# A four-layer graph network on one core: the end of layer 0 in one written order, row terms by sums, late searches in resident chunks' places

## The chip, the core and the metric

The kernel runs on one core of one Trainium2 chip. The metric is device time in microseconds of one execution. An execution is also recorded by the hardware profiler; its times are given from the start of its span. The engines are named PE (TensorE, with PEld for its weight loads), DVE (VectorE), ACT (ScalarE), POOL (GpSimd) and SP (SyncE, which here only issues transfers).

## The reference

`x` is 2708 x 128, `adj` is 2708 x 2708, all in float32. Four layers are applied, each as `x = x + layer(relu(layernorm(x)))`. Layers 0 and 1 are the ones that the change touches:

```
# layer 0: h = relu(layernorm(x)); d = 1/sqrt(rowsum(adj))
z  = leaky_relu(d * (adj @ (d * h)) @ W1 + b1, 0.1)
d2 = max(|z_i|^2 + |z_j|^2 - 2 z_i.z_j, 0)
S  = exp(-sqrt(d2 + 1e-10) / 2), kept for the 4 largest of each row, else 0
A2 = S + adj;  d' = 1/sqrt(rowsum(A2))
x  = x + d' * (A2 @ (d' * h)) @ W2 + b2

# layer 1: h = relu(layernorm(x)); XW = h @ W
s_col, s_row = XW @ a[:128], XW @ a[128:]
den = exp(leaky_relu(s_row_i + s_col_j, 0.01));  num = adj @ den
x  = x + adj @ ((den / num, 0 where num is 0) @ XW)
```

Layers 2 and 3 each multiply `adj` by `h` once more and apply dense weights.

## The kernel before, in words

Nodes are cut into T = 22 tiles of 128 (the last, T-1, has 20 rows) and into six groups of four tiles (the last group has tiles 20 and 21). `adj` comes in transposed, and a chunk is 128 of its rows, 1354 KB. Chunks pass through four rotating places (`big`, tag "big"); the last five, 17 to 21, stay resident in places of their own ("res17" to "res21"). All transfers of chunks go through SP's queue in program order.

Row sums: every chunk is multiplied by ones (L373), while layer 0's node products are made between the chunks (`weighted`).

`aggregate` (L272) is the loop of each multiplication by `adj`. For each chunk that isn't resident it makes six products into six PSUM banks (`acc0` to `acc5`; a float32 product of 128x512 is two passes in the profile); then it adds the resident chunks bank by bank, and calls `done(g)` for each finished bank. `kept` says how many of the last chunks stay in `big`, `back` from which chunk on missing resident chunks are read.

Search: for each tile a strip of 2708 similarities is made by PE (L512, L520), copied by ACT (L527), and searched by DVE: MAX8 finds the eight largest values (L529), FIND_INDEX8 their places (L531). From tile LATE = T-4 on, FIND_INDEX8 is put off (`find_last`, L549). The strips of tiles 18 and 19 lie in two spare places ("U", "Z"), the others in `big`. From the values come `sim`, `deg2`, `dinv2` and the scaled rows `y2` (L577, L579), which are also written to DRAM as `ydr` (L583).

The four nearest rows of each node are added by `add_near` (L600): per tile four indirect gathers from `ydr` on POOL (L604), each of 128 rows, and four DVE terms that add them, weighted by `simd`, to `xs` (L610). Tiles 0 to 14 are added ahead of the aggregation of `y2`, the others within its `done_l0` or after it. 23 buffers (`gath`) take the gathered rows.

`done_l0(g)` (L733) takes a finished bank: ACT copies it (`u2T`, L650), PE transposes it, DVE adds it to `xs` (`add_l0`, L644), and `layernorm_relu` (L203) makes `h1`: moments on DVE (L211, L212), the root on ACT (L213), reciprocal and scale on DVE (L214, L216), RELU on ACT (L221). Then layer 1's row term is made: for groups 0 to 3 by `terms` (L659: transposes of `h1` into `hT`, a product with `rep`, and transposes back), for groups 4 and 5 by `last_terms` (L675: a DVE product with `wrow` and a sum, then PE transposes that spread it into `row_all`). `column_terms` (L703) makes the column term from `hT`; `own_tiles` (L713) compares a group with itself.

Layer 1's attention goes by sorted places: `place(t)` (L813) makes a mask of `row_all` against tile t's row terms on DVE (L844), sums it on ACT (L845) and counts it on PE (L822); `places_of` turns counts into places, and POOL scatters them (L879). `node_terms` at t = 16 finishes the column terms. Between them `total` (L905) adds up chunks weighted by `w_n` (L913), the four of `big` and the five resident ones first, then 13 that are read again. Last, a loop over 22 steps (L1106) fetches rows of `adj` in sorted order into `mov` and writes a table of knots to DRAM.

The program's order on an engine is planned by a scheduler from program order and priorities; `pin(ins)` keeps an instruction in program order among the pinned ones of its engine.

Of the kernel before, what the change touches and what calls it, by code (L numbers as in the profile page):

```python
# [9 lines left out]
F32 = mybir.dt.float32  # L10
# [15 lines left out]
def kernel(  # L26
# [29 lines left out]
    def width(t):  # L56
        return TAIL if t == T - 1 else P
# [15 lines left out]
    def pin(ins):  # L73

        return tc.keep_in_program_order(ins)

    resident = {}
    pools = {}
# [117 lines left out]

    def acc(b):
        return ps_a.tile([P, 512], F32, name=f"acc{b}")

    def span(g):  # L200
        return slice(GROUPS[g][0] * P, min(GROUPS[g][1] * P, N))
# [133 lines left out]
    def weighted(g, part):  # L335
        t0, t1 = GROUPS[g]
        if part == 0:
            p = acc(g % 2)
            for t in range(t0, t1):
                o = (t - t0) * P  # L340
                mm = nc.tensor.transpose(
                    p[:, o : o + width(t)], h0[: width(t), t, :], ident[: width(t), : width(t)]
                )
                if t == t0:
                    pin(mm)
            nc.scalar.copy(h0T[:, span(g)], p[:, : span(g).stop - span(g).start])
            return
        dst, w = ((y1, w1), (hw2, w2))[part - 1]
        p = acc(2 * part + g % 2)
        for t in range(t0, t1):  # L350
            o = (t - t0) * P
            mm = nc.tensor.matmul(
                p[: width(t), o : o + P], h0T[:, cols(t)], w, start=True, stop=True
            )
            if t == t0:
                pin(mm)
        for a, e, n in ((t0, min(t1, T - 1), P), (max(t0, T - 1), t1, TAIL)):
            if a < e:
                (nc.scalar.copy, nc.vector.tensor_copy)[part - 1](
                    dst[:n, a:e, :],  # L360
                    p[:n, (a - t0) * P : (e - t0) * P].rearrange("p (t f) -> p t f", f=P),
                )

    for g in range(NG):
        layernorm_relu(h0, g)
    for i in range(T):
        c = chunk(i)
        w = width(i)
        if 3 <= i < 3 + 3 * NG:
            weighted((i - 3) // 3, i % 3)  # L370
        for b, (k0, n) in enumerate(KBS):
            g = 32 * (b % 4)
            nc.tensor.matmul(  # L373
                sums[b // 4][g : g + 32, :n],
                ones[:w, :32],
                c[:w, k0 : k0 + n],
                start=(i == 0),
                stop=(i == T - 1),
            )
        if i < FIRST:  # L380
            del resident[i]
    sum_rows = lay.tile([P, 1024], F32, name="sum_rows", tag="U")
    for half, p0, p1 in ((0, 0, 128), (1, 0, 32 * (NKB - 5)), (1, 32 * (NKB - 5), 32 * (NKB - 4))):
        n = KBS[4 * half + p0 // 32][1]
# [107 lines left out]
    top_v = res.tile([P, T, 8], F32, name="top_v")  # L492
    top_i = res.tile([P, T, 8], U32, name="top_i")

    LATE = T - 4
    strips = []
    nc.vector.memset(top_v[:, T - 1, :], 0.0)

    def strip(t):
        if LATE <= t < LATE + 2:  # L500
            return lay.tile([P, N], F32, name=f"strip{t}", tag="UZ"[t - LATE])
        return big.tile([P, N + 1], F32, name="strip", tag="big")[:, :N]

    for t in range(T):
# [62 lines left out]
    dinv2 = keep.tile([P, T], F32, name="dinv2")  # L567
    nc.scalar.activation(deg2s, deg2s, AF.Ln)
    nc.scalar.activation(dinv2, deg2s, AF.Exp, scale=-0.5)
    y2 = lay.tile([P, T, D], F32, name="y2", tag="Y")  # L570
    ydr = dram.tile([P * T, D], F32, name="ydr")
    for i in range(2):
        resident[i] = chunk(i)
    for t0, t1 in ((0, T // 2), (T // 2, T)):
        for t in range(t0, t1):
            if t % 5 in (1, 3):
                scaled = nc.scalar.mul(y2[:, t, :], hw2[:, t, :], dinv2[:, t : t + 1])  # L577
            else:
                nc.vector.tensor_scalar(  # L579
                    y2[:, t, :], hw2[:, t, :], dinv2[:, t : t + 1], None, op0=ALU.mult  # L580
                )
        pin(
            nc.sync.dma_start(  # L583
                ydr.rearrange("(p t) f -> p t f", t=T)[:, t0:t1, :], y2[:, t0:t1, :]
            )
        )
    with tc.issue_after(scaled.ins):
        nc.scalar.preload_act_table_set("sqrt_and_others")
    for t in (T - 2, T - 1, *range(LATE, T - 2)):
        find_last(t)  # L590
    row_numbers(P, LATE, T - 1)
    row_numbers(TAIL, T - 1, T)
# [4 lines left out]
        simd, sim, dinv2[:, :, None].to_broadcast([P, T, TOPK]), ALU.mult  # L597
    )

    def add_near(t, late=False):  # L600
        w = width(t)
        for k in range(TOPK):
            g = res.tile([P, D], F32, name="gath", bufs=23)
            nc.gpsimd.indirect_dma_start(  # L604
                out=g[:w, :],
                out_offset=None,
                in_=ydr[:, :],
                in_offset=bass.IndirectOffsetOnAxis(ap=near_u[:w, t, k : k + 1], axis=0),
            )
            term = nc.vector.scalar_tensor_tensor(  # L610
                xs[:w, t, :],
                g[:w, :],
                simd[:w, t, k : k + 1],
                xs[:w, t, :],
                op0=ALU.mult,
                op1=ALU.add,
            )
            if late and k == 0:
                pin(term)

# [6 lines left out]
    def vec(name, n=T, dt=F32):  # L629
        return keep.tile([P, n], dt, name=name)  # L630
# [17 lines left out]
    def to_x1(g, s2):  # L648
        k0, n = KBS[g]
        nc.scalar.copy(u2T[:, k0 : k0 + n], s2[g][:, :n])  # L650
        node_product(u2T, None, g, add_l0)
# [20 lines left out]
            )  # L672
        nc.vector.tensor_copy(r_nat[:, t0:t1], r_ps[0][:, t0:t1])

    def last_terms(g):  # L675

        t0, t1 = GROUPS[g]
        k0, n = KBS[g]
        prod = res.tile([P, 4, D], F32, name="prod")
        nc.vector.tensor_tensor(  # L680
            prod[:, : t1 - t0, :],
            h1[:, t0:t1, :],
            wrow[:, None, :].to_broadcast([P, t1 - t0, D]),
            ALU.mult,
        )
        e = min(t1, T - 1)
        nc.vector.tensor_reduce(r_nat[:, t0:e], prod[:, : e - t0, :], AX.X, ALU.add)
        if e < t1:
            nc.vector.tensor_reduce(
                r_nat[:TAIL, e:t1], prod[:TAIL, e - t0 : t1 - t0, :], AX.X, ALU.add  # L690
            )
        p = ps_s.tile([P, 512], F32, name="ps")
        for t in range(t0, t1):
            w = width(t)
            o = (t - t0) * P
            nc.tensor.transpose(
                p[:, o : o + w], r_nat[:w, t : t + 1].to_broadcast([w, P]), ident[:w, :w]
            )
        return nc.scalar.copy(row_all[:, k0 : k0 + n], p[:, :n])

    c_ps = []

# [25 lines left out]
            nc.vector.tensor_tensor(o, o, eq, ALU.subtract)  # L728


    late = {0: (15,), 1: (16,), 2: (17,), 3: (18, 19), 4: ()}

    def done_l0(g, s2):  # L733
        to_x1(g, s2)
        if g < NG - 1:
            layernorm_relu(h1, g)
            for t in late[g]:
                add_near(t, late=True)
        if 1 <= g < NG - 1:
            terms(g - 1)  # L740
        if g == NG - 1:
            last_terms(g - 1)
        if g > 2:
            column_terms(g - 3)
        if g in (2, 3):
            own_tiles(g - 2, res)

    for t in range(15):
        add_near(t)
    aggregate(y2, done_l0, lambda i: spread(y2, nc.sync) if i == 4 else None, kept=4)  # L750
    transposed(hT, h1, NG - 2, nc.scalar.copy)
    column_terms(NG - 3)
    for t in range(GROUPS[-1][0], T):
        add_near(t, late=True)
    layernorm_relu(h1, NG - 1)
    last_row = last_terms(NG - 1)
    transposed(hT, h1, NG - 1, nc.scalar.copy)
    column_terms(NG - 2)

    with tc.issue_after(last_row.ins):  # L760
        tables = nc.scalar.preload_act_table_set("natural_log_exp_and_others")
# [23 lines left out]
        return top  # L785

    rmax = node_max("rmax", r_nat, r_ps[0][:, 256:384])
    r_n = vec("r_n")
    nc.vector.tensor_scalar(r_n, r_nat, rmax, None, op0=ALU.subtract)
    w_n = vec("w_n")  # L790
# [130 lines left out]
    early = {todo[len(here) + n]: total_chunk(todo[len(here) + n], n) for n in range(2)}  # L921

    def node_terms():
        column_terms(NG - 1)
        nc.vector.tensor_copy(c_nat[:, : T - 1], c_ps[0][:, : T - 1])
        nc.vector.tensor_copy(c_nat[:TAIL, T - 1 :], c_ps[0][:TAIL, T - 1 : T])
        cmax = node_max("cmax", c_nat, c_ps[0][:, 384:512])
        nc.vector.tensor_scalar(cmx, cmax, rmax, -1.0, op0=ALU.add, op1=ALU.mult)
        c_n = vec("c_n")
        nc.vector.tensor_scalar(c_n, c_nat, rmax, None, op0=ALU.add)  # L930
        nc.vector.tensor_scalar(hb, c_n, 0.0, -0.495, op0=ALU.max, op1=ALU.mult)
        nc.scalar.activation(s_n, c_n, AF.Exp, scale=0.99)
        nc.scalar.activation(sig, hb, AF.Exp)
# [4 lines left out]
    for t in range(T):  # L938
        place(t)
        if t % 4 == 3 or t == T - 1:  # L940
            places_of(t // 4)
        if t in (2, 5, 8, 11):
            own_tiles(2 + t // 3, spare)
        if t == 16:
            node_terms()
        if 1 <= t <= len(here) + 4 or t in (15, 16, 18, 20):
            total(done)
            done += 1
# [124 lines left out]
            )  # L1073

    weights(0)


    xw = lay.tile([P, T, D], F32, name="xw", tag="Y")
# [299 lines left out]
```

## Time and profile before

| | us |
|---|---|
| three timed runs | 1194.0, 1194.6, 1188.3 |
| median | 1194.0 |
| the profiled execution | 1289.2 |
| its span | 1287.3 |
| row sums, to the first product of `aggregate(y1)` | 0 to 93.5 |
| `aggregate(y1)` and the search | 93.5 to 337.3 |
| `aggregate(y2)`, to the first finished bank | 337.3 to 506.4 |
| end of layer 0, to the first mask of `place` | 506.4 to 552.3 |
| places and totals, to the first table product | 552.3 to 619.7 |
| table, attention, layers 2 and 3 | 619.7 to 1287.3 |

A line of the timeline gives the start, the time of a run of like instructions, the engine, the line of the program, the operation, output and inputs, and how often; in brackets stands the idle time before it and what ended it. A row of the table of stretches gives the stretch, its length, the busy time and instructions of PE, PEld, DVE, ACT and POOL, PE's granted clock, the DMA share and GB/s. The slices of the page cut the span in 40, 32 us each.

### The profile page before, as it was taken

Reading aid. Unit: us, or ns where it says so; the run is one execution under the profiler, and the core shown is the slowest. Engines: PE = TensorE matmul, PEld = TensorE weight load, DVE = VectorE, ACT = ScalarE, POOL = GpSimd, SP = SyncE. Lnnn points to the kernel's source line nnn. Section 1 sums busy time; section 2 is a strip of 40 time slices with the busy share of each in tenths; the row PEclk is TensorE's granted clock in tenths of the full one; section 3 lists DMA queues with packets and bytes.
Section 4 is the critical chain, followed back from the end, with each engine's and each line's share of the span. In section 5 each row is a group of like instructions: output and inputs, shape, how many; then the busy total and the mean of one; then the engine's idle time right before and its main releaser. Section 6 shows DMA issues by size and latency. Waiting matters only on the chain. (4 is left out here: it accounts for less than half of the span.)

```text
span 1287.3 us, 10181 instructions
## 1 busy us (share of the span) xinstructions
PE 1056.8 (82%) x3603; PEld 499.3 (39%) x3603; DVE 561.4 (44%) x1177; ACT 409.7 (32%) x636; POOL 245.7 (19%) x211
## 2 busy tenths in 40 slices
PE   4879999999763379797677771787879999999998
PEld 1324444444221134454333330333334445545444
DVE  2020026999832001783466663899970012104003
ACT  3100014544300000475567644687840012003000
POOL 4000000000277700134211103577500000000000
PEclk9989999999875579788899896698889999999999
DMA  9997800001553361256999997999949945761841
GB/s 344 422 383 276 302 3 1 1 1 43 212 202 96 94 253 50 90 233 245 274 406 395 345 348 269 423 414 419 417 184 395 326 164 181 265 245 54 306 159 43
DMA packets 38800, 298.76 MB, mean 232 GB/s; under 512 B 6735, under 2 KB 9710, under 8 KB 12290
## 3 DMA queue, kind: packets, MB, share of 16 engines
q1 hardware_dynamic: 24798, 203.76, 42.0%
q0 software_dynamic: 13952, 94.36, 19.7%
q8 instruction: 28, 0.46, 0.1%
q14 instruction: 22, 0.18, 0.0%
HBM read 265.76 MB, written 32.87 MB: 232 GB/s over the span
## 5 line engine op out<-in xcount | busy, mean ns | idle before, releaser
L284 PE MATMUL acc<-chunk,y 128*128 128x512 f32 (+1 forms) x408 | 180.3, 591 | 74.7 <-issue 58.4
L1213 PE MATMUL acc<-hi,xw 128*128 128x512 f32 (+3 forms) x264 | 124.2, 634 | 57.8 <-DVE hi L1203 57.8
L1106 PE MATMUL acc<-mov,wt 128*128 128x512 f32 (+1 forms) x264 | 115.4, 592 | 40.7 <-DMA mov<-in_adj_dram,src_u 39.2
L284 PE MATMUL acc<-chunk,h 128*128 128x512 f32 (+1 forms) x384 | 148.3, 542 | 0.0
L604 POOL DMA_INDIRECT gath<-ydr,near_u x88 | 83.8, 952 | 337.5 <-DMA ydr<-y 245.9
L284 PEld LDWEIGHTS acc<-chunk,y 128*128 128x128 f32 x408 | 79.5, 205 | 175.5 <-issue 162.0
L512 PE MATMUL acc<-zT 128*128 128x512 f32 (+2 forms) x264 | 112.7, 559 | 0.4 <-ACT strip L527 0.3
L1213 PEld LDWEIGHTS acc<-hi,xw 128*128 128x128 f32 (+1 forms) x264 | 55.7, 220 | 126.3 <-issue 66.1
L1110 DVE COPY mov<-acc 2x512 f32<-2x512 f32 x126 | 74.3, 611 | 61.1 <-PE acc L1106 60.5
L284 PEld LDWEIGHTS acc<-chunk,h 128*128 128x128 f32 x384 | 68.6, 190 | 73.2 <-issue 73.1
L1106 PEld LDWEIGHTS acc<-mov,wt 128*128 128x128 f32 x264 | 52.1, 205 | 103.8 <-issue 82.3
L527 ACT COPY strip<-acc 128x512 f32<-128x512 f32 (+2 forms) x132 | 60.7, 556 | 61.0 <-issue 35.8
L284 PE MATMUL acc<-chunk,attended 128*128 128x512 f32 x192 | 73.1, 542 | 2.5 <-DMA chunk<-in_adj_dram 2.5
L1145 POOL DMA_INDIRECT lo<-table,lo_u x22 | 58.0, 2638 | 68.6 <-issue 41.1
L1111 ACT COPY knots<-acc 128x512 f32<-128x512 f32 x88 | 50.2, 590 | 62.9 <-DVE mov L1110 56.4
L1195 ACT ACTIVATE hi<-hi,lam 128x2708 f32<-128x2708 f32 (+3 forms) x24 | 56.5, 2363 | 35.6 <-issue 26.7
L1191 DVE SCALAR_TENSOR_TENSOR hi<-lo,lam,hi 128x2708 f32<-128x2708 f32 (+3 forms) x24 | 67.1, 2801 | 1.0
L1203 DVE SCALAR_TENSOR_TENSOR hi<-row_all,inv_s,hi 128x2708 f32<-128x2708 f32 (+3 forms) x24 | 67.0, 2797 | 0.4 <-ACT hi L1196 0.4
L512 PEld LDWEIGHTS acc<-zT 128*128 128x128 f32 (+1 forms) x264 | 45.0, 185 | 51.7 <-issue 41.9
L529 DVE MAX8 top_v<-strip 128x8 f32<-128x2708 f32 (+1 forms) x22 | 64.4, 2967 | 0.4 <-ACT strip L527 0.4
L650 ACT COPY u2T<-acc 128x512 f32<-128x512 f32 (+1 forms) x6 | 3.2, 533 | 168.3 <-PE acc L284 168.2
L1196 ACT ACTIVATE hi<-hi,hb 128x2708 f32<-128x2708 f32 (+3 forms) x24 | 56.5, 2361 | 0.7
(281 smaller groups left out, 1179.5 us busy)
## 6 DMA issues: line engine op xcount, KB each, us to landing
chunk<-in_adj_dram SPq DMA_DIRECT2D x108, 1354.0 KB
table<-knots SPq DMA_DIRECT2D x20, 1354.5 KB
res<-in_adj_dram SPq DMA_DIRECT2D x9, 1354.0 KB
chunkY<-in_adj_dram SPq DMA_DIRECT2D x2, 1354.0 KB
chunkU<-in_adj_dram SPq DMA_DIRECT2D x2, 1354.0 KB
res<-in_adj_dram SPq DMA_DIRECT2D x8, 211.6 KB
ydr<-y SPq DMA_DIRECT2D x2, 704.0 KB
gath<-ydr,near_u POOLq DMA_INDIRECT x88
```

The lines of the kernel that those rows point to most:

```text
L284: nc.tensor.matmul(out[b][:, :n], y[r, i, :], chunk(i)[r, k0 : k0 + n], start=(i == 0), stop=(i == T - 2),)
L512: mm = nc.tensor.matmul(zz[b][:w, :n], zT[:, cols(t)], zT[:, k0 : k0 + n], start=True, stop=False)
L527: copied = nc.scalar.copy(s[:w, k0 : k0 + n], zz[b][:w, :n])
L529: nc.vector.max(top_v[:w, t, :], s[:w, :])
L604: nc.gpsimd.indirect_dma_start(out=g[:w, :], out_offset=None, in_=ydr[:, :], in_offset=bass.IndirectOffsetOnAxis(ap=near_u[:w, t, k : k + ...
L1106: nc.tensor.matmul(p[:, :n], wt[:, t, :], moving[t][:, k0 : k0 + n], start=True, stop=True)
L1110: nc.vector.tensor_copy(moving[t + 1][:2, k0 : k0 + n], p[:2, :n])
L1145: nc.gpsimd.indirect_dma_start(out=dst[:w, :], out_offset=None, in_=table[:, :], in_offset=bass.IndirectOffsetOnAxis(ap=idx[:w, t : t + 1] ...
L1191: nc.vector.scalar_tensor_tensor(num, lo[:w, c], kap, num, op0=ALU.mult, op1=ALU.add)
L1195: nc.scalar.activation(num, num, AF.Ln, scale=sc)
L1203: nc.vector.scalar_tensor_tensor(att[:w, c], row_all[:w, c], inv_s[:w, t : t + 1], att[:w, c], op0=ALU.max, op1=ALU.mult,)
L1213: nc.tensor.matmul(py[b][:, :n], xw[:w, t, :], att[:w, k0 : k0 + n], start=(t == T - 1), stop=(t == T - 2),)
```

## The change

It has these parts.

- Row sums: chunk T-1 is taken ahead of T-2, and after each of the last six chunks PE makes three products of constants that nobody reads (`warm`).
- Search: LATE is T-5. The strips of tiles 17, 20 and 21 take the places of the resident chunks 17, 18 and 19, which are then dropped and read again in `aggregate(y2, ...)` from its sixth chunk on (`back=5`).
- 16 unread products follow the search; four chunks instead of two are asked for ahead of `ydr`, which is written in three parts instead of two.
- Tile T-1's gathers: the four lists of 20 rows are copied into one list of 128 (`near_p`, `simd_p`, at partitions 0, 32, 64 and 96) by eight small transfers from ACT's queue; one gather and one PE product with `four_w` take their place.
- End of layer 0: banks 4 and 5 are no longer worked off one by one in `done_l0`, but after the loop, in an order written out for PE, DVE and ACT (`Ordered` pins each instruction).
- Groups 3 to 5 get their row terms by sums; their `hT` and column terms are made after `rmax` and in `node_terms`, and `own_tiles(1)` moves to `place`.
- 14 unread products follow `weights(0)`, ahead of the table loop.

```
+    class Ordered:          # every call is pinned
+        def __getattr__(self, name):
+            return lambda *a, **k: pin(getattr(self.engine, name)(*a, **k))
+    pe, dve, act = Ordered(nc.tensor), Ordered(nc.vector), Ordered(nc.scalar)
...
+    def warm(p, n):
+        for _ in range(n):
+            pin(nc.tensor.matmul(p, ident_b, ident_b[:, None, :].to_broadcast([P, 4, P]), start=True, stop=True))
...
-    for i in range(T):
+    for n_, i in enumerate([*range(T - 2), T - 1, T - 2]):
...
+        if n_ >= T - 6:
+            warm(acc(0), 3)
...
-    LATE = T - 4
+    LATE = T - 5
...
     def strip(t):
-        if LATE <= t < LATE + 2:
-            return lay.tile([P, N], F32, name=f"strip{t}", tag="UZ"[t - LATE])
+        if t in (LATE, T - 2, T - 1):
+            i = T - L0_RES + (LATE, T - 2, T - 1).index(t)
+            del resident[i]
+            return res_rows.tile([P, N + 1], F32, name=f"strip{t}", tag=f"res{i}")[:, :N]
+        if t > LATE:
+            return lay.tile([P, N], F32, name=f"strip{t}", tag="UZ"[t - LATE - 1])
...
+    warm(acc(5), 16)
...
-    for i in range(2):
+    for i in range(4):
         resident[i] = chunk(i)
-    for t0, t1 in ((0, T // 2), (T // 2, T)):
+    for t0, t1 in ((0, 9), (9, 17), (17, T)):
...
+    near_p = res.tile([P, 1], U32, name="near_p")
+    simd_p = res.tile([P, 1], F32, name="simd_p")
...
+    for k in range(TOPK):
+        for dst, src in ((near_p, near_u), (simd_p, simd)):
+            nc.scalar.dma_start(dst[32 * k : 32 * k + TAIL, :], src[:TAIL, T - 1, k : k + 1])
...
+    def last_near():
+        g = gathered(near_p)
+        dve.tensor_scalar(four_w, four_w, simd_p, None, op0=ALU.mult)
+        p = ps_s.tile([P, 512], F32, name="ps")
+        pe.matmul(p[:TAIL, :P], four_w[:, :TAIL], g, start=True, stop=True)
+        return p
...
-    late = {0: (15,), 1: (16,), 2: (17,), 3: (18, 19), 4: ()}
+    late = {0: (15,), 1: (16,), 2: (17,), 3: (18,)}
+    complete = []
     def done_l0(g, s2):
+        if g >= NG - 2:
+            complete.append(s2[g])
+            return
         to_x1(g, s2)
-        if g < NG - 1:
-            layernorm_relu(h1, g)
-            for t in late[g]:
-                add_near(t, late=True)
-        if 1 <= g < NG - 1:
+        layernorm_relu(h1, g)
+        for t in late[g]:
+            add_near(t, dve)
+        if g:
             terms(g - 1)
-        if g == NG - 1:
-            last_terms(g - 1)
-        if g > 2:
-            column_terms(g - 3)
-        if g in (2, 3):
-            own_tiles(g - 2, res)
+        if g == 2:
+            own_tiles(0, res)
...
+    aggregate(y2, done_l0, ..., kept=4, back=5)
+    # E4, E5 = groups 4, 5: ACT copies both banks, PE transposes both
+    column_terms(0)
+    add_near(T - 3, dve)
+    x1(E4)
+    for t in range(*GROUPS[E4]):
+        moments(t)
+    roots(E4)
+    x1(E5)
+    normed(E4)
+    p = last_near()
+    prod = row_sums(E4 - 1)
+    natural(E4 - 1, prod)
+    as_row(E4 - 1)
+    column_terms(1)
+    column_terms(2)
+    dve.tensor_tensor(xs[:TAIL, T - 1, :], xs[:TAIL, T - 1, :], p[:TAIL, :P], ALU.add)
+    moments(T - 1)
+    add_near(T - 2, dve)
+    moments(T - 2)
+    roots(E5)
+    prod = row_sums(E4)
+    normed(E5)
+    natural(E4, prod)
+    as_row(E4)
+    natural(E5, row_sums(E5))
+    last_row = as_row(E5)
...
     rmax = node_max("rmax", r_nat, r_ps[0][:, 256:384])
+    for g in range(E4 - 1, NG):
+        transposed(hT, h1, g, nc.scalar.copy)
...
     def node_terms():
-        column_terms(NG - 1)
+        for g in range(E4 - 1, NG):
+            column_terms(g)
...
-        if t in (2, 5, 8, 11):
-            own_tiles(2 + t // 3, spare)
+        if t in (1, 2, 5, 8, 11):
+            own_tiles(1 + (t + 1) // 3, spare)
...
     weights(0)
+    warm(acc(5), 14)
```

`x1(g)` adds the transposed banks to `xs` on DVE; `moments(t)`, `roots(g)` and `normed(g)` are the steps of `layernorm_relu`, split so that they can be set in order; `row_sums`, `natural` and `as_row` are the steps of the former `last_terms`.

## The prediction

> **What bounds the kernel now.** I read the chip line first, then the slices, the groups, the timeline of each turn between stages, and the waits. The chain that ended last reaches back only to 921 us, so all that the change touches has to be read from the timeline. The slices show one stretch unlike the rest:
>
> ```profile
> ## 2 busy tenths in 40 slices
> PE   4879999999763379797677771787879999999998
> ...
> PEclk9989999999875579788899896698889999999999
> ```
>
> Slices 12 to 15 (about 370 to 480 us) are the second aggregation of layer 0 (`aggregate(y2, ...)`, L284), which should keep PE full. The table of stretches (PE, PEld, DVE, ACT, POOL busy, clock, DMA share, GB/s) says what happened:
>
> ```profile
> 337.00:369.00 32.00, 31.40 (x76) 14.43 (x76) 20.49 (x46) 3.96 (x10) 19.02 (x20) 0.93 0.79 301
> 369.00:461.00 92.00, 32.22 (x37) 10.54 (x37) 14.64 (x42) 0.00 (x0) 60.09 (x64) 0.52 0.30 91
> 461.00:501.00 40.00, 36.74 (x96) 17.24 (x99) 0.00 (x0) 0.00 (x0) 0.00 (x0) 0.96 0.62 243
> ```
>
> For 92 us PE took one product per 1.4 us instead of 0.43, with nothing to wait for ("issue"), and DMA idled. The same loop over layer 0's first matrix gives its normal length: its chunk part runs from 93.51 to 173.56, 80.05 us; here it runs from 337.28 to 500.71, 163.4 us. So this execution holds 83.4 us that a normal one doesn't. It took 1289.2 us, the three timed runs 1188 to 1195: 83.4 of the 95 us between are this stretch. I therefore read every time after it less 83.4 ("corrected"), and the sum below against 1289.2 - 83.4 = 1205.8, which stands 1% above the median of 1194; differences are carried over one to one. The correction matters: in the profile the gathers look free, since they finished while PE crawled; in a normal run they don't.
>
> The turn before it, from the search for the nearest rows to the aggregation:
>
> ```profile
> 325.17 5.84 DVE L529 MAX8 top_v<-strip 128x8 f32<-128x2708 f32 x2
> 327.30 0.38 PE L520 MATMUL acc<-sq_rows,ones_b 3*20 3x512 bf16 x2
> 331.40 2.96 DVE L529 MAX8 top_v<-strip 20x8 f32<-20x2708 f32 x1
> 337.28 31.40 PE L284 MATMUL acc<-chunk,y 128*128 128x512 f32 x76 [9.60 <-DVE y L579]
> 338.47 1.56 SPq L583 DMA_DIRECT2D ydr<-y  x2
> 344.20 1.03 POOL L604 DMA_INDIRECT gath<-ydr,near_u  x1 [245.88 <-DMA ydr<-y]
> ```
>
> DVE bounds the search: from the first MAX8 at 216.8 to 334.36 it never pauses, 40 instructions (22 MAX8, 18 FIND_INDEX8) of 2.94 us. PE and ACT are done with the last strip at 328.9. The end of the layer:
>
> ```profile
> 506.35 0.59 ACT L650 COPY u2T<-acc 128x512 f32<-128x512 f32 x1 [165.37 <-PE acc L284]
> ...
> 548.05 0.29 DVE L211 BATCH_NORM_STATS2 ln_st<-xs 128x6 f32<-128x128 f32 x1
> ...
> 552.28 1.56 DVE L844 TENSOR_SCALAR mask<-row_all,r_nat 128x2580 bf16<-128x2580 f32 x1 [0.78 <-ACT row_all L699]
> ```
>
> The first mask of layer 1 starts at 552.28, 45.9 us after the first finished bank; corrected, 422.9 and 468.9. PE's clock between 529 and 555 is 0.56: the chain DVE, ACT, PE is passed back and forth there, and none is full.
>
> **What the Trainium skill says.** "TensorE: Matmul & The Clock Gate", Part 1: an idle window of about 3.4 us halves PE's clock, and as long a busy one restores it. The trace agrees: after its 9.6 us of idleness at 337.28 the weight loads stand 0.85 us apart until 341.4, then 0.43; at 93.5 the same for 5.4 us. So the two starts lose 2.0 and 2.7 us. The same part warns that the gate was seen "stuck at K=1/4 for 50+µs"; 92 us at under a third of the rate is like that, but no run here shows the cause. "DMA: Bandwidth & Descriptors", Issuing engines are not separate DMA queues: transfers of all queues share the same 16 engines. Here too: from 348 to 364, gathers and chunks together, the DMA share is 1.0 at about 395 GB/s.
>
> **The change part by part.**
>
> *Row sums (stage to 93 us).* Chunk T-1 is read before T-2, and each of the last six chunks is followed by three unread products. 18 bf16 products of 128x512, at 0.216 us by the TensorE page's Back-to-back issue gap (no run here shows them), come to 3.9 us on PE, hidden in its waits for DMA in this stage (28 us at L373), except for the last three, 0.65 us, beside the DVE copy of 0.69. What they buy is the 2.7 us of cold start at 93.5. The last two chunks land 3 us apart, at half clock; reordering may save part of a microsecond or nothing. The idle gap of 3.1 us before the last full chunk may still let the clock fall. Between +0.7 (the last three uncovered, no warmth) and -3.3; I take -2.0.
>
> *Search.* LATE goes from T-4 to T-5: one FIND_INDEX8 (2.94) leaves the path to `dinv2` and joins the finds after it. DVE could end at 331.4, but the last strip is only copied at 328.9, so the last MAX8 ends at 331.8. Gain 2.5 (1 to 2.9). The five late finds hold DVE as long as before, to about 351.5, covered by gathers and PE; `near_u` of the late tiles is read some 70 us later (uncovered, 2.9).
>
> *Unread products before `y2`.* 16 products, 3.5 us at the same price, from 328.9 to 332.4, leaving under 3 us until y2: warm start, -2.0 (0 to -2.0). They end ahead of dinv2, so they delay nothing.
>
> *Chunks.* The strips of tiles 17, 20 and 21 take the places of resident chunks 17 to 19, so `big` is free early: four chunks lie ready instead of two, but three must be read again. In the loop DMA carries 13 + 3 = 16 chunks. Beside gathers a chunk costs 1.386 MB / 345 GB/s = 4.02 us (395 less the gathers' 50), PE 4.51 us (76.7 / 17). Loads start when chunk 0 is released, at 334.8 + 4.5 = 339.3. With `back=5` the extras queue on SP behind chunks 5, 7 and 9, so chunk 10 is the tenth load: 339.3 + 2 + 40.2 = 381.5, wanted at 379.9. Cost +1.6; from below 0, from above +8, at 4.4 us a chunk and more.
>
> *Gathers.* 88 become 85: tile T-1's four of 20 rows become one, with a product against `four_w`. They start one every 1.255 us, and land 2.7 after their start (the sixtieth starts at 418.51, its term runs at 421.21). The third `ydr` issue (0.33 us on SP) is met by the smaller last piece. First gather at about 341.6; T-3's last lands at 443.6, the very last at 449.9 (before: 456.3). The eight small copies on ACT's queue, 0.33 us each by SP's issues, the three adds for `four_w` and the memsets fall at 352 to 360, where ACT has nothing else (uncovered, 2.6).
>
> *End of layer 0.* First bank: 422.9 - 2.5 - 2.0 + 1.6 = 420.0. The loop's banks and groups 0 to 3 keep their course; groups 4 and 5 wait for all banks (+22.5), then copies, transposes: `x1` can begin at about +26 = 446, by which time T-3's terms (443.6) are in. On DVE, from the rows: x1 of six tiles 1.6, moments of four 1.7, reciprocal and scale 0.34, four_w 0.25, row sums of group 3 1.38, the add 0.28, moments 0.44, four terms 1.1, moments 0.44: 7.5, so 453.6, past the last gather at 449.9. Then root, scale, two RELUs, product, sums, transposes, copy: from the moments to the mask it is now 3.7; group 4's two sums hide partly in these waits, +0.7. Mask at 458.0, 38.0 us after the first bank against 45.9: -7.9. Pinned orders let one late gather hold everything behind it (`add_near(T-3)` has x1, moments and both roots queued behind it on DVE, and ACT's RELUs and PE's transposes behind those). I take -7.0; bounds -9.5 and 0.
>
> *What moves past the mask.* `transposed` of groups 3 to 5 (20 PE passes, three ACT copies: 1.5 us), eight more tiles of `column_terms` (16 passes, eight in 1.05 to 1.87 us: 2.1 to 3.7, at t = 16), `own_tiles(1)` (2.2 us on DVE, 18 of 20 us busy from 560 to 580); also early pieces of `own_tiles` that filled DVE's gaps at 540 to 547. Much lies beside totals and chunk reads, but place ends in a chain DVE, PE, POOL up to 605. Between 0 and +6; I take +3.0.
>
> *Products before the table loop.* 14 products, 3.0 us warm and 6.0 at half clock, run in PE's wait of 6.5 us for the first `mov`; the first step took 7.9 us cold against 6.0 for the second. DMA is full in that loop (share 1.01), so I take -1.0 of at most 2.3.
>
> Sum: -2.0 - 2.5 - 2.0 + 1.6 - 7.0 + 3.0 - 1.0 = **-9.9**: 1184 us from the median of 1194. About 0.5% (6 us) is what a measurement of this kernel can tell from no change.
>
> **The rivals.**
>
> *Moved, not removed* (0.19). The tail's gain returns as work behind the mask, and the warm starts don't hold: tail -5, place +6, search -2.5, warm 0, reload +1.6: about 1194. For it: DVE is 18/20 busy just there. Against it: PE idles 1.9 and 3.5 us at 585 and 592.
>
> *Reloads make DMA the bound; slower* (0.15). If a chunk beside gathers costs r, the sixteenth lands at 341.3 + 16 r, and PE wants it at 407.0. At 4.02 that is in time, at 4.8 it costs 11.5, the whole gain; from 5.2 (17 us late) the kernel is slower by over 0.5%, near 1201. For it: the margin is half a microsecond per chunk, and gathers use 20% of DMA (420 to 440). Against it: 360 to 364 shows 384 GB/s beside gathers.
>
> *The change does what it says* (0.66): 1176 to 1188. That the throttled stretch enters timed runs would give about 1270; none of three shows it, and I leave it outside the range.
>
> **How the numbers follow.** All good ends together give about 1174, all bad ones about 1207; with few parts at their ends at once, 1176 to 1199 holds 8 in 10, the rivals' near parts included. Faster 0.66, same 0.19, slower 0.15 are the three cases.
>
> **What would show it.** Right: weight loads 0.43 us apart from the first at both aggregations; 17 FIND_INDEX8 before `sim`; 85 gathers; no DMA wait over 2 us at L284 in the y2 loop; from the first u2T copy to the first mask some 38 us; from that mask to the first table product about 70 us (now 67.4). Wrong: chunk waits of many microseconds there; DVE idle on `gath` after the banks are done; a stretch from mask to table over 74 us.

## The result, and the profile after

The change makes no measurable difference: median 1191.7 us against 1192.5 us for the kernel before (20 runs each), ratio 0.9997 (95% interval 0.9978 to 1.0015). A second comparison, run f1 below, gave 1.0005 (0.9989 to 1.0021). The forecast was 1184 us.

The profiled execution of the change took 1191.5 us, its span 1189.7. On some chips PE is held within `aggregate(y2)`, whatever the kernel: for 80 to 93 us it takes one pass of a product per 2.8 us or so, where it else takes one per 0.43, as in the first profile of before. I call these held chips. So the change is set against a profile of before from an unheld chip, run f4 (1195.8 us, span 1194.0). The slices of the change, from the page:

```profile
## 2 busy tenths in 40 slices
PE   4899999999997997977878718778798999999998
...
PEclk9999999999999896989988957888899999999999
```

No throttled stretch is left, but the thirteenth slice (357 to 387 us) shows PE at 7, in a loop that should fill it. The timeline of the turn into the loop and of the end of the layer, in the change:

```profile
325.54 2.97 DVE L558 MAX8 top_v<-strip 20x8 f32<-20x2708 f32 x1 [0.29 <-ACT strip L556]
325.55 3.61 PE L216 MATMUL acc<-ident_b 128*128 128x512 bf16 x16 [1.22 <-ACT strip L556]
331.42 29.10 PE L305 MATMUL acc<-chunk,y 128*128 128x512 f32 x72 [2.26 <-DVE y L609]
338.19 1.03 POOL L646 DMA_INDIRECT gath<-ydr,near_u  x1 [242.25 <-DMA ydr<-y]
361.12 9.33 PE L305 MATMUL acc<-chunk,y 128*128 128x512 f32 x24 [0.59 <-DMA chunk<-in_adj_dram]
373.26 9.32 PE L305 MATMUL acc<-chunk,y 128*128 128x512 f32 x24 [2.82 <-DMA chunk<-in_adj_dram]
386.86 34.92 PE L305 MATMUL acc<-chunk,y 128*128 128x512 f32 x84 [4.27 <-DMA chunk<-in_adj_dram]
...
427.36 0.59 ACT L704 COPY u2T<-acc 128x512 f32<-128x512 f32 x1 [92.23 <-PE acc L305]
...
465.69 1.56 DVE L984 TENSOR_SCALAR mask<-row_all,r_nat 128x2580 bf16<-128x2580 f32 x1 [0.29 <-ACT row_all L84]
```

The same places in before, run f4:

```profile
336.57 79.47 PE L284 MATMUL acc<-chunk,y 128*128 128x512 f32 x204 [9.60 <-DVE y L579]
...
421.61 0.59 ACT L650 COPY u2T<-acc 128x512 f32<-128x512 f32 x1 [81.35 <-PE acc L284]
...
466.83 1.56 DVE L844 TENSOR_SCALAR mask<-row_all,r_nat 128x2580 bf16<-128x2580 f32 x1 [0.78 <-ACT row_all L699]
```

Read them together. The loop starts 5.2 us earlier, and the end of the layer takes 38.3 us instead of 45.2. Between the two, before runs its 204 chunk products in one piece; the change is stopped three times, each time ahead of a chunk, 7.7 us in all, and is twice at a low clock (at its start and after the last stop: 29.10 us for six chunks and 34.92 for seven, where g1 below takes 4.6 us per chunk). Its first bank therefore comes 5.75 us later than in before, and the first mask of layer 1 only 1.1 us earlier.

The stages, each from one profiled execution on an unheld chip (us; "chunk part" is from the first product of `aggregate(y2)` to the first of tile T-1; "end" from the first u2T copy to the first mask; "to table" from that mask to the first table product):

| | before f4 | change | f1 | f2 | f3 | g1 | h1 | h2 | g3 | g4 |
|---|---|---|---|---|---|---|---|---|---|---|
| start of y2 | 336.6 | 331.4 | 333.5 | 331.1 | 333.6 | 332.9 | 329.7 | 331.3 | 332.7 | 332.1 |
| chunk part | 79.4 | 90.3 | 89.5 | 85.2 | 82.5 | 77.4 | 77.4 | 86.1 | 77.4 | 80.2 |
| end | 45.2 | 38.3 | 38.3 | 38.2 | 38.5 | 43.1 | 43.5 | 44.9 | 45.2 | 38.7 |
| to table | 61.0 | 63.3 | 65.2 | 63.9 | 63.1 | 63.9 | 64.1 | 60.7 | 60.3 | 65.8 |
| table loop | 153.6 | 150.0 | 151.3 | 148.7 | 152.6 | 148.0 | 156.4 | 156.0 | 159.5 | 152.8 |

Change against f4: start -5.2, chunk part +10.9, end -6.9, to table +2.4, table loop -3.6, the rest -1.8: together -4.2, as the spans (1189.7 and 1194.0). f1 against f4: -3.1, +10.1, -6.9, +4.2, -2.3, -3.0: -0.9, as the spans again. The one term with the wrong size is the chunk part.

What SP's queue waited for between 325 and 470 us, in the change (queue and line, releaser: total us, times, longest):

```profile
SPq L98 <- PE acc L305: 38.7, 9, 7.8
SPq L613 <- DVE y L609: 19.0, 2, 18.6
SPq L98 <- DMA simd_p<-simd: 11.8, 1, 11.8
SPq L98 <- DMA chunk<-in_adj_dram: 6.1, 2, 3.8
```

and the timeline of what SP and ACT's queue issued in that time:

```profile
339.94 2.79 SPq L98 DMA_DIRECT2D chunk<-in_adj_dram  x2
342.82 0.38 SPq L98 DMA_DIRECT2D res<-in_adj_dram  x1
...
349.02 1.32 ACTq L638 DMA_DIRECT2D simd_p<-simd  x1
350.44 1.49 ACTq L638 DMA_DIRECT2D near_p<-near_u  x2
...
355.06 0.80 SPq L98 DMA_DIRECT2D chunk<-in_adj_dram  x2
355.96 0.61 SPq L98 DMA_DIRECT2D res<-in_adj_dram  x1
```

After the first re-read chunk SP issues nothing for 11.8 us, and what it waits for is one of the eight small transfers on ACT's queue, with which its next load shares no data. The compiled program shows the tie: all transfers of SP's and ACT's queues take turns, in the order of the program, over eight completion counters, and each waits until the last user of its counter is done. The eight small ones stand between the loads of chunks 5 and 6, so chunk 6's load waits for the first of them; that one can't be issued before the late searches have given `simd` and `near_u`. "DMA: Bandwidth & Descriptors" of the Trainium skill, "Why a DMA increments its semaphore by 16 and not by 1", gives the reason for such a rule: two transfers in flight on one semaphore can release a waiter early, hence "One semaphore per in-flight slot". By its section "Queues, rings and completion order" the completion write lands only after every earlier write of that DMA engine, across queues. The trace agrees on the tie: the semaphore for which SP stands is that of the first small transfer, whose last count comes at 355.00, and SP goes on at 355.06. The order of the writes it doesn't show; that 80 bytes, issued from 349.0 to 350.3, took until then, with chunks under way, would fit.

### The profile page after: what moved, and what is told of

The parts are those of the page before. It is cut to its first block, busy times and chain, and to the rows that moved or that the text cites. A ratio compares the mean times of both kernels' runs of the same rounds, so it can differ in the third digit from the quotient of the medians.

```text
span 1189.7 us, 10297 instructions
## 1 busy us (share of the span) xinstructions
PE 1039.3 (87%) x3651; PEld 495.2 (42%) x3651; DVE 562.5 (47%) x1181; ACT 408.9 (34%) x636; POOL 241.6 (20%) x208
## 5 line engine op out<-in xcount | busy, mean ns | idle before, releaser
L305 PE MATMUL acc<-chunk,y 128*128 128x512 f32 (+1 forms) x408 | 161.8, 559 | 11.7 <-DMA chunk<-in_adj_dram 7.7
L646 POOL DMA_INDIRECT gath<-ydr,near_u x84 | 80.3, 956 | 267.5 <-DMA ydr<-y 242.2
L305 PEld LDWEIGHTS acc<-chunk,y 128*128 128x128 f32 x408 | 75.7, 196 | 98.1 <-issue 90.9
L541 PE MATMUL acc<-zT 128*128 128x512 f32 (+2 forms) x264 | 112.7, 559 | 0.4 <-ACT strip L556 0.3
L1355 PEld LDWEIGHTS acc<-hi,xw 128*128 128x128 f32 (+1 forms) x264 | 55.8, 221 | 126.6 <-issue 66.7
L1248 PEld LDWEIGHTS acc<-mov,wt 128*128 128x128 f32 x264 | 51.3, 202 | 91.7 <-issue 77.9
L556 ACT COPY strip<-acc 128x512 f32<-128x512 f32 (+2 forms) x132 | 60.7, 556 | 61.0 <-PE acc L549 30.8
L1115 ACT ACTIVATE sg<-row_all,c_nat 128x2708 bf16<-128x2708 f32 (+1 forms) x22 | 56.2, 2555 | 0.1
```

The source lines that it names most:

```text
L305: nc.tensor.matmul(out[b][:, :n], y[r, i, :], chunk(i)[r, k0 : k0 + n], start=(i == 0), stop=(i == T - 2),)
L541: mm = nc.tensor.matmul(zz[b][:w, :n], zT[:, cols(t)], zT[:, k0 : k0 + n], start=True, stop=False)
L556: copied = nc.scalar.copy(s[:w, k0 : k0 + n], zz[b][:w, :n])
L646: nc.gpsimd.indirect_dma_start(out=g[: idx.shape[0], :], out_offset=None, in_=ydr[:, :], in_offset=bass.IndirectOffsetOnAxis(ap=idx, axis=0),)
L1248: nc.tensor.matmul(p[:, :n], wt[:, t, :], moving[t][:, k0 : k0 + n], start=True, stop=True)
L1355: nc.tensor.matmul(py[b][:, :n], xw[:w, t, :], att[:w, k0 : k0 + n], start=(t == T - 1), stop=(t == T - 2),)
```

## The experiments

My theory after the result: the gains came as forecast and were given back in `aggregate(y2)`, where SP stands behind the small transfers and the three re-read chunks are read ahead of chunks that are wanted sooner. Rivals: the added bytes alone, wherever they stand; the gathers; a loss behind the mask.

**Held chips: e1 to e4.** e1 is before, unchanged. e2:

```
-            nc.scalar.dma_start(dst[32 * k : 32 * k + TAIL, :], src[:TAIL, T - 1, k : k + 1])
+            nc.vector.tensor_copy(dst[32 * k : 32 * k + TAIL, :], src[:TAIL, T - 1, k : k + 1])
```

e3 (e4 is e2 and e3 together; `strip` goes back to that of before with it, and the comments are added here):

```
-    LATE = T - 5          # strips of 17, 20, 21 in resident places
+    LATE = T - 4          # as before: 18, 19 in "U", "Z"; 20, 21 in big
...
-    for i in range(4):
+    for i in range(2):
...
-    for t in range(LATE, T):
+    for t in (T - 2, T - 1, *range(LATE, T - 2)):
...
-    aggregate(y2, ..., kept=4, back=5)
+    aggregate(y2, ..., kept=4)
```

e1: 

> The kernel before, unchanged, for a profile without the throttled stretch. If the correction of 83.4 us was right: y2 chunk part (first product of aggregate(y2) to the tile T-1 products) about 80 us, first u2T copy about 85.6 us after the first product, first mask about 45.9 us after that copy, mask to first table product about 67.4, table to end about 667. If other stages of that profile were long too, one of the last two comes out shorter by several us; then the sum of 1205.8 was measured against a wrong own time.

e2: 

> The change with its eight small transfers (near_p, simd_p) made as eight small DVE copies instead; nothing else is changed. Theory (SP's queue stands behind these transfers for 8 to 12 us, and PE then waits for chunks): SP no longer waits on simd_p, the y2 chunk part takes 82 to 85 us instead of 90.3, PE's waits for chunks there fall from 10.7 to under 5 us, and the kernel gains 5 to 8 us on the change (ratio to before about 0.994). Rival (the three re-read chunks alone fill DMA, so it does not matter when SP asks): chunk part stays at 89 to 91 us, kernel within 2 us of the change.

e3: 

> The change without its search part: LATE is T-4 again, tiles 20 and 21 lie in big, no resident chunk is dropped or read again, two chunks are asked for ahead; the eight small transfers stay. One FIND_INDEX8 (2.94 us) returns to the path. Theory (both the wait of SP and the re-read chunks are needed for the loss): SP still waits for simd_p, but three chunks (12 us of DMA) less are wanted, so the chunk part takes 78 to 83 us; the start comes 2.5 us later; net 5 to 9 us faster than the change. Rival (SP's wait alone makes the loss): chunk part 86 to 90 us, and the kernel is no faster than the change.

e4: 

> Both together: small DVE copies, and no chunk dropped or read again. Theory: PE waits under 2 us for chunks, chunk part 76.7 to 79 us, start 2.5 us later than in the change; kernel 8 to 11 us faster than the change (ratio to before 0.991 to 0.994), about what the prediction gave for the whole change. Rival (the gathers, not SP or the re-read chunks, hold the chunks up): chunk part 84 us or more, within 4 us of the change.

e1 took 1274.7 us, before beside it 1280.1 in the median; e2, e3 and e4 had ratios to before of 0.9892 (0.9850 to 0.9934), 0.9954 (0.9932 to 0.9976) and 0.9946 (0.9925 to 0.9966). Their chunk parts are 157.7, 159.5, 162.0 and 162.0 us: PE was held in all four, here in e2 (stretch, length, busy PE, PEld, DVE, ACT, POOL, clock, DMA share, GB/s):

```profile
365.00:455.00 90.00, 33.27 (x42) 10.81 (x40) 14.69 (x44) 0.00 (x0) 59.67 (x63) 0.54 0.35 116
```

In the held stretch itself no chunk is late (PE waits for a chunk for 1.5 us in e3 and 1.8 in e4 ahead of it, and for 3.3 to 4.0 just after it in e2 to e4), so the theories are not told apart. e1 shows something else: from mask to table it takes 67.1 us, as in the first profile of before, against 61.0 in f4. So the held chips are also slower after the stretch.

**Copies or re-reading: f1 to f4, on one unheld chip.** f1 is the change, f2 is e2's kernel, f3 is e4's, f4 is before.

f1: 

> The change itself, beside the kernel before and the three below on one chip. Where PE runs at full rate through aggregate(y2): within 0.2% of before, chunk part about 90 us with some 10 us of waits for chunks. Where PE is held at one product per 1.4 us for some 90 us in that loop, as in the first profile of before: PE then never waits for re-read chunks, so by the theory (the loop gives the gain back for lack of chunks) the change is 10 to 14 us faster than before (ratio about 0.990); by the rival (the gain is lost behind the mask, in place) it is no faster there either.

f2: 

> The change with its eight small transfers made as small DVE copies. At full rate, theory (SP stands behind those transfers): chunk part 82 to 85 us, 5 to 8 us faster than the change (ratio to before about 0.994); rival (the three re-read chunks fill DMA anyway): within 2 us of the change. With PE held back: within 2 us of the change either way.

f3: 

> Small DVE copies, and LATE at T-4 with no chunk dropped or read again. At full rate, theory: chunk part 77 to 80 us, 8 to 11 us faster than the change (ratio to before 0.991 to 0.994); rival (the gathers hold the chunks up): 84 us or more. With PE held back: 3 to 7 us slower than the change, since one FIND_INDEX8 is back on the path and nothing is saved in the loop.

f4: 

> The kernel before, for a profile on this chip. At full rate: chunk part 80 to 82 us, first u2T copy to first mask 45.9, mask to first table product about 67, table to end about 663.

f1 has ratio 1.0005; its chunk part is 89.5 us. f2: 0.9949 (0.9928 to 0.9970), 6.9 us by the medians faster than f1, chunk part 85.2, no wait of SP on `simd_p`. That is what the theory expected, at the edge of its range: the small transfers cost the change 4.3 us in the loop. But f2 still waits; its products (f2, timeline of PE):

```profile
331.08 36.85 PE L305 MATMUL acc<-chunk,y 128*128 128x512 f32 x96 [2.26 <-DVE y L609]
372.04 11.96 PE L305 MATMUL acc<-chunk,y 128*128 128x512 f32 x24 [4.11 <-DMA chunk<-in_adj_dram]
384.33 32.04 PE L305 MATMUL acc<-chunk,y 128*128 128x512 f32 x84 [0.33 <-DMA chunk<-in_adj_dram]
```

It loses 4.1 us ahead of chunk 8 and then 2.6 at a low clock (11.96 us for two chunks instead of 9.3), and all the same has to wait a little for chunk 10. f3: 0.9938 (0.9913 to 0.9963), no wait for a chunk, but 82.5 instead of the 77 to 80 expected: it starts cold (12.39 us for its first two chunks) and waits 1.7 us for a late search (`top_i`), whose strip still lies in `big`. f4 came out close to what was expected, but for 61.0 us from mask to table instead of 67.

**The place of the re-reading: g1 and g2.** g1, on f2:

```
-    aggregate(y2, ..., kept=4, back=5)
+    aggregate(y2, ..., kept=4, back=16, first=3)
```

g2 is the change with its eight transfers moved, `dma_start` and all, into `to_x1(0)`, behind the first bank's copy.

g1: 

> Small DVE copies as in f2, and the three dropped chunks are asked for after the last chunk of the loop (back=16, first=3) instead of behind chunks 5, 7 and 9. The same bytes are read. They are wanted from about 86 us after the loop's start on, asked for at about 58, and take 12 us. At full rate, theory (it is where they stand in SP's order, ahead of chunks that are wanted sooner, that costs): no chunk waits, chunk part 77 to 79 us from a start at 331 to 333, kernel 5 to 7 us faster than f2 (ratio to before 0.988 to 0.990). Rival (the added bytes themselves cost): still 83 us or more in the chunk part or as much lost at the resident chunks, within 2 us of f2. Where PE is held back in the loop: no difference to f2.

g2: 

> The change with its eight small transfers kept as transfers on ACT's queue, but issued after the first bank's copy to u2T, so behind all chunk loads in the order of the program. Theory (the small transfers take completion counters in turn with SP's loads, and the next load has to wait until the first of them is done): SP no longer waits on simd_p, chunk part about 85 us as with DVE copies, kernel 3 to 7 us faster than the change (up to 3 us of ACT's time and a later last gather may be lost at the end of the layer). Rival (eight transfers of 20 rows cost by themselves, wherever they stand): within 2 us of the change. Where PE is held back: within 3 us of the change either way.

g1: ratio 0.9934 (0.9901 to 0.9967); repeated as h4, 0.9934 (0.9908 to 0.9961). The same bytes are read, and the loop is whole (h4, timeline of PE):

```profile
331.97 77.50 PE L305 MATMUL acc<-chunk,y 128*128 128x512 f32 x204 [2.26 <-DVE y L609]
```

7.8 us less in the chunk part than f2: not the bytes, but their place in SP's order was the cost. The kernel gains some 2 us by the ratios instead of the 5 to 7 expected, with overlapping intervals: the end takes 43.1 us instead of 38.2. g2: chunk part 85.3, as f2, and SP doesn't wait for `simd_p`; so a small transfer holds SP only by its place in the program. The kernel is at 0.9985 (0.9959 to 1.0012), a smaller gain than the 3 to 7 us expected; 1.2 us of it is a longer end (39.5), the rest is not resolved.

**Which of the two, and the search part by itself: h1, h2.** h1 is the change with g1's line alone, the transfers left where they are. h2 is before with the change's `LATE`, `strip`, four chunks ahead, order of late searches and `back=5`.

h1: 

> The change with one edit: the dropped chunks are read again after the last chunk (back=16, first=3); the eight small transfers stay where they are. Theory that both are needed for the loss (SP stands still to about 355, but without the re-read chunks in between it has caught up before PE wants the next one): chunk part 77 to 80 us, kernel as fast as g1. Rival (the small transfers cost their 4 to 6 us whatever the order of the chunks): chunk part 82 to 85 us, kernel 3 us or more slower than g1.

h2: 

> The kernel before with the search part alone: LATE at T-5, strips of 17, 20 and 21 in resident places, four chunks ahead, re-reading behind chunks 5, 7 and 9; no unread products, no small transfers, old end of layer 0. Theory: aggregate(y2) starts 3 to 4 us earlier, its chunk part takes 85 to 88 us instead of 79.4, so the part by itself makes the kernel 2 to 4 us slower (ratio 1.001 to 1.004). Rival (the forecast's own terms, -2.5 and +1.6): about 1 us faster, chunk part 81 us.

h4: 

> g1 again (small DVE copies, late re-reading), beside the three above on one chip: ratio to before 0.992 to 0.994, chunk part 77 to 78 us, first u2T copy to first mask 42 to 44 us with DVE waiting 4 to 5 us for gathered rows.

h1: chunk part 77.4, as h4; 126.6 us from the start of y2 to the mask (h4: 126.5). With the re-reading late the small transfers cost nothing in the loop, though SP still stands behind them: it asks for chunk 6 at 343.7 and for chunk 7 only at 353.2, just after the first of them is done (352.9), where h4 has 4.5 us between the two. SP has caught up before PE wants the chunk, so both together make the larger loss, as the theory said. The times are 0.9961 (0.9942 to 0.9980) and 0.9934; the profiles differ in the table loop (156.4 and 150.9), which neither edit touches, so that remainder isn't explained. h2: 1.0032 (1.0009 to 1.0055), chunk part 86.1 us:

```profile
331.35 39.55 PE L284 MATMUL acc<-chunk,y 128*128 128x512 f32 x96 [7.09 <-DVE y L583]
371.49 9.32 PE L284 MATMUL acc<-chunk,y 128*128 128x512 f32 x24 [0.60 <-DMA chunk<-in_adj_dram]
383.78 33.74 PE L284 MATMUL acc<-chunk,y 128*128 128x512 f32 x84 [2.96 <-DMA chunk<-in_adj_dram]
```

By itself, and with no small transfer at all, the search part makes the kernel slower.

**Tail and unread products: g3, g4.** g3 is before with the change's row sums, search part, unread products and g1's late re-reading; its gathers, end of layer 0 and row terms are those of before. g4 is g1 without any `warm`.

g3: 

> The kernel before with the search part, row-sum order, four chunks ahead and all unread products of the change, with the late reading again of g1, and with the end of layer 0, its gathers and the row terms as before. Forecast's terms: start and loop as in g1 (-6 to -9 us against before), tail 45 us instead of 38, and mask to first table product 61 instead of 64: 3 to 5 us slower than g1, ratio to before 0.992 to 0.995. Rival (the tail's gain is given back wholly behind the mask): equal to g1.

g4: 

> g1 without any unread product (neither in the row sums, nor before y2, nor ahead of the table loop). By the forecast's terms (2.0 + 2.0 + 1.0, half of the first being the warm start) 3 to 5 us slower than g1; by a rival (the clock is lost anyway or regained elsewhere, since other work waits for DMA there) within 1 us of g1.

g3: 0.9968 (0.9949 to 0.9987); by the medians 3.9 us slower than g1, in the range expected, but not for the reason expected. From the start of y2, mask and first table product come at 128.3 and 188.6 us in g3, at 126.2 and 190.1 in g1: once the chunks are on time, the new end is 2 us shorter, and the work that it moved past the mask takes more than that. From the mask to the table's last product the old order took 214.6 to 219.7 us in three profiles, the new one 211.9 to 220.4 in ten, so what remains is within their scatter. g4: 0.9933 (0.9912 to 0.9955), equal to g1, as the rival had it: without the unread products the chunk part is 2.8 us longer (80.2), and the end 4.4 us shorter.

**What takes over: h3, i1, i2.** h3 is g1 without `add_near(T - 2, dve)`; i1 is g1 with `range(1, 15)` for `range(15)`; i2:

```
-    add_near(T - 3, dve)
     x1(E4)
-    for t in range(*GROUPS[E4]):
+    for t in range(GROUPS[E4][0], T - 3):
         moments(t)
-    roots(E4)
     x1(E5)
+    add_near(T - 3, dve)
+    moments(T - 3)
+    roots(E4)
```

h3: 

> g1 without the four gathers and terms of tile T-2: these rows get no neighbour term. If the row of gathers (85 at 1.25 us from 339 on) sets the end of layer 0 once the chunks come in time, the last gather starts 5 us earlier, the first mask comes 3.5 to 5 us earlier than in g1 (about 455), and the kernel gains 3 to 5 us on g1. If the written order of the end does (38 us from the first u2T copy), the mask moves by under 2 us.

i1: 

> g1 without the four gathers and terms of tile 0 (these rows get no neighbour term), so that every later gather, T-3's too, starts four places earlier. In g1 DVE stood 4.1 us before T-3's second term, with x1, moments and both roots queued behind it. Theory (the row of gathers sets the end through that wait): the wait goes, the mask comes 3 to 5 us earlier after the start of aggregate(y2) than in g1 (126.5 us there), and the stage behaves as after f2, where 38.3 us lay between first copy and mask. Rival (DVE's own work, or PE's transposes of banks 4 and 5, come just as late): under 1.5 us.

i2: 

> g1 with T-3's four terms moved in DVE's written order behind x1 of both groups and the moments of tiles 16 to 18; nothing else. Theory: 2.9 us of DVE work (four and two x1 terms 1.7, three moments 1.2) fill the wait of 4.1 us, so the mask comes 2 to 3 us earlier (about 124 us after the start of aggregate(y2)), ratio to before 0.991 to 0.993. Rival (transposes of banks 4 and 5 come no earlier than T-3's rows): under 1 us.

h3: 0.9958 (0.9939 to 0.9977); the mask comes 125.6 us after the start of y2, in h4 126.5. My expectation of 3.5 to 5 us was wrong. I had taken away the wrong gathers (DVE's timeline, h4 first, then h3):

```profile
443.55 0.61 DVE L84 SCALAR_TENSOR_TENSOR xs<-gath,simd,xs 128x128 f32<-128x128 f32 x2 [4.09 <-DMA gath<-ydr,near_u]
```

```profile
441.56 0.61 DVE L84 SCALAR_TENSOR_TENSOR xs<-gath,simd,xs 128x128 f32<-128x128 f32 x2 [2.95 <-DMA gath<-ydr,near_u]
```

These are terms of tile T-3, at the head of DVE's written order, 111.6 us after the start of y2 in h4 and 111.4 in h3; T-2's gathers come after them. i1 (0.9881, 0.9834 to 0.9928) and i2 (0.9923, 0.9892 to 0.9954) were to test that wait. Both fell on a held chip (chunk parts 150.8 and 158.0 us), where DVE waited for no gathered row at the end, so they tell nothing of it. That T-3's rows set the end in g1 is what the trace says; no run shows it.

The trace also says why these rows are late, and it is not the length of the row of gathers. In h4, three gathers up to 436.6 us land 2.6 us after their issue; the next two, T-3's last, take 6.5 (count, size or median time to landing, from the DMA views of h4 for 434.0 to 436.6 us and for 436.7 to 439.5):

```profile
gath<-ydr,near_u POOLq DMA_INDIRECT x3, 2.6
```

```profile
chunkY<-in_adj_dram SPq DMA_DIRECT2D x1, 1354.0 KB
chunkU<-in_adj_dram SPq DMA_DIRECT2D x1, 1354.0 KB
gath<-ydr,near_u POOLq DMA_INDIRECT x2, 6.5
```

The two chunks are the first loads for `total`, which SP asks for as soon as the loop has released their places: in h4 105.0 and 106.8 us after the start of y2, between T-3's gathers. In f2, with its late loop, SP asks for them 112.7 us after it, when T-3's rows have landed, and the end takes 38.2 us; in g4 107.7 us after it, and the end takes 38.7. No run moves these two loads, so this stays a reading of the traces.

## Why the prediction was wrong

- **Row sums (-2.0): mostly not seen.** The first product of `aggregate(y1)` stands at 91.1 and 91.5 us in the change, at 92.9 in f4, at 91.7 in g4 without the products and at 90.6 in h2 with the old row sums, so its start is within the scatter. The warm start itself would show after it. In f1 three weight loads are 0.43 us apart, then four 0.85: the clock still falls. Only h1, h3 and i1 have all loads 0.43 apart, and they take 238.6 us from y1's first product to y2's; the change takes 240.3 and g4, without the products, 240.3 too.
- **Search (-2.5) and warm start of y2 (-2.0): right.** From y1's first product to y2's, 243.7 us became 240.3 and 242.0, and 240.8 in h2 with the search part alone; g1's chunk part is 2.8 us under g4's. The change's own profile starts cold nevertheless (0.85 apart to 334.1), f1 and g1 do not.
- **Chunks (+1.6): the step that failed.** f1 measured +10.1 together with the warm start, so about +12, where the bound was +8 (the change's own profile, which starts cold, +10.9). The sum for the tenth load, chunk 10, was wrong in its start above all. I let loads begin 4.5 us after the start of y2, when chunk 0 is released; in f2 SP asks for the first at 339.6, 8.5 us after it, because the spreading of tile T-1's `y2` stands ahead in its queue, waits 3.1 us for `ydr` and takes 2.4 to issue. The pace was wrong by less: chunk 10 landed in f2 at 384.2, so (384.2 - 339.6 - 2) / 10 = 4.26 us per load, not 4.02. SP had asked for it at 363.4; the loads stood in line for DMA, whose share is 1.01 or more from 346 to 384. So chunk 10 came 53.1 us after the start of y2, where the forecast has PE want it at 45.1: +8.0 instead of +1.6, 4.0 more by the start and 2.4 by the pace. f2 lost 7.8 against g1. The waits for chunks 8 and 10 and the low clock between them are how that delay shows.
- **Eight small copies (nothing): failed too.** I asked only what ACT had to do. They take 0.73 us or more each on ACT's queue, not 0.33, which is indeed covered; but SP's next load had to wait 11.8 to 13.1 us for the first. That makes the other 4.3 of the 12 us (f1 against f2): PE gets chunk 10 2.6 us later than in f2, and then takes 33.74 us for the last seven chunks instead of 32.04. With the re-reading late they cost the loop nothing (h1).
- **End of layer 0 (-7.0): right.** 38.3 us where I had 38.0, from 45.2. But here it goes with the late loop: with the chunks on time and a warm start it is 43, with DVE waiting for T-3's rows, which the forecast had in time by 2.4 us. That g1's mask, at 459.1, is so near to the forecast's 458.0 is luck: its loop starts 1.9 us before the forecast's 334.8 (those times leave out the -2.0 of the row sums) and is 2.1 shorter to the first bank, its end is 5.1 longer.
- **Moved past the mask (+3.0): right in size**, +2.4 and +4.2. The stretch itself is 61.0 us without a held PE, not 67.4: subtracting 83.4 us corrected the loop (79.4 measured, 80.0 assumed), not what came after.
- **Table loop (-1.0):** -3.6 and -2.3, but profiles of one order scatter by some 8 us (148.0 in g1, 156.4 in h1), so this term isn't measured.
- **Smaller slips.** In the held stretch of before the passes start some 2.8 us apart, not 1.4; the 83.4 us don't rest on it. The rival's sum at 4.8 us per chunk gives 11.1 us, not 11.5.

The rival "reloads make DMA the bound" had the right place, the wrong test (the sixteenth chunk's landing) and no part for SP's wait; by itself it is real (h2, and the full DMA in f2). The time landed where "moved, not removed" had it, by luck, for it came another way: nothing was lost behind the mask that had not been allowed for.

The best version is g1, at 0.9934, which is f2's copies and two arguments; f3 and g4 are as fast.

## What to carry to other kernels

Count for each load of a queue when it is wanted and when it can land, load by load, before putting others ahead of it; what is wanted last is read last, even when its place has long been free. A small transfer on another queue is not beside the loads if the program shares completion counters: look at what stands after it in program order, or copy on an engine. And when one chain has been shortened, ask what was running just under it, and what its earlier end sets off: here DVE's wait for gathered rows took back about 5 us of the 8 that the loop released.

## What the runs showed that I had not expected

On two of the five chips that the runs name (e and i), PE was held in this loop, from about 365 us on, in every kernel profiled there (chunk part 151 to 163 us instead of 77 to 90), and from mask to table these profiles are slower too (67 to 73 us instead of 60 to 66). On the other three no such stretch appeared. Each chip was used once, so chip and time of use aren't told apart, and the cause stays open. A comparison across the two kinds means nothing. And a held loop hides what chunks cost: there e2, which reads three chunks again, has a shorter chunk part than e4, which doesn't (159.5 and 162.0 us); on an unheld chip the same two kernels, f2 and f3, have 85.2 and 82.5.
